# The last part of a convolution, attention and expert kernel issued in a written-out cyclic order

## The chip, the cores and the metric

The kernel runs on one core of a Trainium2 chip. The metric is the device time of one execution in microseconds. The kernel before took 6046.41 us, the median of three runs from 6041.91 to 6047.18. The core has five engines that work in parallel, each through its own list of instructions in order: TensorE (PE; its weight loads are shown apart as PEld), VectorE (DVE), ScalarE (ACT), GpSimd (POOL) and SyncE (SP), which in this kernel issues nearly all DMA transfers. An engine waits for another through semaphores.

## The reference

The input is 32 images of 128 channels and 64 x 64 pixels, float32. What is computed, cut to what matters:

```
# layer 0: group norm, then a convolution through learned butterfly transforms
x = x + conv(group_norm(x), weight, kd1, kd2, k11, k12, k21, k22)
#   x_f  = K11 . x . K12            (64 x 64 complex matrices along h and w)
#   prod[b, o, h, w] = sum_i x_f[b, i, h, w] * w_f[o, i, h, w]
#   out  = real(K21 . prod . K22)
# layer 1, on tokens t[b, pixel, channel]
k, v   = ln(t) @ Wk.T + bk, ln(t) @ Wv.T + bv
scores[b, e, f] = sum over pixels of k[b, pixel, e] * v[b, pixel, f]     # 128 x 128, one per image
t      = t + (softmax(scores / sqrt(32)) over f, applied to the channels of ln(t))
p      = softmax(ln(t) @ router_w + router_b)      # 8 experts, the best 2 kept, renormalised
t      = t + sum over the kept experts of gate * (ln(t) @ expert_w[e] + expert_b[e])
```

The attention matrix of an image is thus formed from all its 4096 tokens before it is applied to any of them; `ln` is a layer norm over the channels, taken anew for the experts.

## The kernel before, in words

The kernel has three parts, each of them a list of operations on tiles that a planner (class `Plan`, line 25) orders and then issues.

Part one transforms each image along w and h and leaves the spectrum in DRAM (`xf`). Part two goes over the 64 frequencies along w, mixes channels with the transformed weights and leaves the product in DRAM (`pf`). Part three, from line 853 on, is the one that is changed. It goes over the 32 images. For each image b it

- loads eight pieces `r0` to `r7` of the product (`load_r`, line 881; two DMAs of 256 KB each, on SP, line 887) and the input image `x` (`load_x`, line 877; 2 MB, on SP, line 879). A piece lies in one of ten buffers: pool `rp` with eight and `rp2` with two;
- transforms back along w: `w0` to `w7` on TensorE read one piece each (line 903, tile `pu`), and two copies to `u` for each half follow on ScalarE (`wo{e}_0`, `wo{e}_1`, line 913). All `w` share one PSUM tile of two banks, so a `w` waits for the `wo` of the one before;
- transforms back along h: `h0` to `h3` on TensorE (line 925, tile `py`), added to the image on VectorE (`ho0` to `ho3`, line 933). For the first two images these two steps are cut in halves (`w{e}_0`, `w{e}_1`, `h{g}_0`, `h{g}`; lines 946 and 965) in other PSUM buffers;
- turns the image to tokens in eight groups: `pt` on TensorE, `to` on ScalarE, `sa` (statistics) on VectorE; then `va`, `pwa` (a power on POOL) and `na` give the first layer norm;
- normalises (`xg`, ScalarE), forms the Gram matrix (`pg`, TensorE), and goes through a chain of small operations to the attention matrix (`gs pb t1 pb2 sm pr sr sn pc prx`);
- applies it to three token groups at a time: `pp` (TensorE), `at` (ScalarE), `ad` (VectorE, with the statistics of the second norm);
- norms again (`vb`, `pwb` on POOL, `nb`) and computes the router: `lg l2 f1 f2 f3 f4 f5 gt`, nearly all on VectorE, where `f1` and `f3` find the best and the second expert and `gt` makes the gates;
- runs the experts: for each of eight groups `xn` (normalise, ScalarE), `px` (transpose, TensorE) and `xT` (copy, ScalarE); for each of 32 token tiles two products `pe{i}_0`, `pe{i}_1` (TensorE, line 1324), each weighed by its gates on VectorE (`m{i}_0`, `m{i}_1`, line 1335); `s` on POOL sums the experts of two token tiles into the tokens; at last `st` (transpose back, TensorE), `so` (copy, ScalarE, line 1376) and the store to DRAM, which `so` issues on SP (line 1377).

Several images are in work at once: while the experts of image b run, image b + 1 is in its attention and image b + 2 or b + 3 in its transform back. `pe` has three PSUM buffers, and the tiles `px pt st pg pb pc pp` share three more.

Which operation comes when is the planner's choice. Each is added with an engine, a guessed duration, a due time and what must come before it (`after`); tokens of limited number (`take`, `free`) stand for buffers. `Plan.run` plays the program through with those guesses: each engine takes of its ready operations that with the earliest due time whose tokens are there. Due times are `SLOT` (114 us) times a position in images, shifted by a table for each kind of operation:

```
    def add(b, key, engine, us, at, run, after=(), take=(), free=(), late=0.0):
        names = [k if isinstance(k, tuple) else (b, k) for k in after]
        at += SHIFT.get(key.rstrip("0123456789_"), 0.0)
        made[b, key] = plan.add(
            engine, us, SLOT * at, run, [made[k] for k in names if k[0] >= 0], take, free, late
        )
```

The order that comes out is the order in which all operations are issued, and so the order of each engine's instructions. Loads and stores share the list of SP: a load of `r` waits there for its buffer, a store for the copy of `so`.

Of the kernel before, what the change touches and what calls it, by code (L numbers as in the profile page):

```python
# [19 lines left out]
NT = NPIX // P  # L20
# [4 lines left out]
class Plan:  # L25
# [12 lines left out]
    def run(self):  # L38
        ops, room = self.ops, self.room
        left = [len(set(o[4])) for o in ops]  # L40
        then = [[] for _ in ops]
        for i, o in enumerate(ops):
            for j in set(o[4]):
                then[j].append(i)
        ready = {o[0]: [] for o in ops}
        for i, o in enumerate(ops):
            if not left[i]:
                heapq.heappush(ready[o[0]], (o[2], i))
        busy = {e: False for e in ready}
        events, order, now = [], [], 0.0  # L50
        while True:
            for e, heap in ready.items():
                if busy[e]:
                    continue
                passed = []
                while heap:
                    due, i = heapq.heappop(heap)
                    take = ops[i][5]
                    if all(room[k] > 0 for k in take):
                        for k in take:  # L60
                            room[k] -= 1
                        order.append(i)
                        busy[e] = True
                        heapq.heappush(events, (now + ops[i][1], 0, i))
                        break
                    passed.append((due, i))
                for p in passed:
                    heapq.heappush(heap, p)
            if not events:
                break  # L70
            now, kind, i = heapq.heappop(events)
            engine, us, due, run, after, take, free, late = ops[i]
            if kind == 0:
                busy[engine] = False
                heapq.heappush(events, (now + 0.15 + late, 1, i))
            else:
                for k in free:
                    room[k] += 1
            for j in then[i]:
                if (kind == 0) == (self.quick and ops[j][0] == engine):  # L80
                    left[j] -= 1
                    if not left[j]:
                        heapq.heappush(ready[ops[j][0]], (ops[j][2], j))
        assert len(order) == len(ops)
        self.length = now
        for i in order:
            ops[i][3]()

# [2 lines left out]
def kernel(  # L91
# [16 lines left out]
    B = x.shape[0]  # L108
# [707 lines left out]
    NG = 4  # L816
# [12 lines left out]
    def prepare():  # L829
# [20 lines left out]
        nc.tensor.matmul(pe[:, 0:NE], om, prx[0][:, P + NE : QX], start=True, stop=True)  # L850
        nc.vector.tensor_scalar_mul(rws, pe[:, 0:NE], float(P))

    plan = Plan({"cv": 1, "pe": 3, "tl": 3, "r": 10, "x": 2, "xg": NG, "xn": 2, "xT": 2, "tm": 2, "so": 2, "gate": 2})
    SLOT = 114.0

    SHIFT = {
        "ad": -0.15, "at": -0.25, "f": 0.71, "gs": -1.97, "gt": 0.71, "h": -0.24, "ho": -3.5, "kvp": 3.43,
        "kvq": -0.45, "l": 0.71, "lg": 3.61, "m": -0.32, "na": -1.87, "nb": -0.81, "pb": -1.97, "pc": -1.97,
        "pe": 0.16, "pg": -0.08, "pp": 0.19, "pr": -1.97, "prx": -1.97, "pt": -0.23, "pwa": -1.87, "pwb": 3.61,
        "px": 0.15, "r": -0.04, "s": 0.08, "sa": 1.29, "sm": -1.97, "sn": -1.97, "so": 2.13, "sr": -1.97,  # L860
        "st": 1.1, "t": -1.97, "to": 0.06, "va": -1.87, "vb": 3.61, "w": 0.28, "x": -0.68, "xT": -0.68,
        "xg": 0.21, "xn": 2.42,
    }
    made = {}

    def add(b, key, engine, us, at, run, after=(), take=(), free=(), late=0.0):


        names = [k if isinstance(k, tuple) else (b, k) for k in after]
        at += SHIFT.get(key.rstrip("0123456789_"), 0.0)  # L870
        made[b, key] = plan.add(
            engine, us, SLOT * at, run, [made[k] for k in names if k[0] >= 0], take, free, late
        )


    def transfers(b):
        def load_x():
            xs[b] = xp.tile([P, HW, HW], F32, tag="x", name=f"y{b}")
            nc.sync.dma_start(xs[b].rearrange("c h w -> c (h w)"), xv[b])

        def load_r(e):
            def run():
                i = 8 * b + e
                ring, tag = (rp, "r") if i % 10 < 8 else (rp2, "r2")
                t = rs[b, e] = ring.tile([P, 16 * n], F32, tag=tag, name=f"r{b}_{e}")
                for r in range(2):
                    nc.sync.dma_start(t[r * n : (r + 1) * n], pfv[b, e, r])
            return run

        for e in range(8):  # L890
            add(
                b, f"r{e}", "SP", 0.2, b - 0.5 + 0.08 * e, load_r(e) if b else (lambda: None), take=("r",),
                late=5.0 if b else 0.0,
            )
        add(b, "x", "SP", 0.1, b + 0.2, load_x if b else (lambda: None), take=("x",), late=12.0 if b else 0.0)

    def conv(b):
        def w_inverse(e):
# [79 lines left out]
        if b < 2:  # L978
            for e in range(8):
                at = b + 0.08 * e  # L980
                for oh in range(2):
                    add(
                        b, f"w{e}_{oh}", "PE", 0.95, at + 0.04 * oh, w_inverse_piece(e, oh),
                        [f"r{e}"] + [(b - 1, f"h{k}") for k in range(4)], ("pe",), ("r",) if oh else (),
                    )
                    add(
                        b, f"wo{e}_{oh}", "ACT", 0.65, at + 0.04 * oh, w_out_piece(e, oh), [f"w{e}_{oh}"], (), ("pe",),
                    )
            for g in range(4):
                for k in range(2):  # L990
                    at = b + 0.68 + 0.07 * g + 0.035 * k
                    h, ho = (f"h{g}", f"ho{g}") if k else (f"h{g}_0", f"ho{g}_0")
                    add(
                        b, h, "PE", 1.05, at, h_inverse_piece(2 * g + k),
                        [f"wo{e}_{oh}" for e in range(8) for oh in range(2)] + ([f"h{g}_0"] if k else []), ("pe",),
                    )
                    add(b, ho, "DVE", 0.7, at, h_out_piece(2 * g + k), [h, "x"] + ([f"ho{g}_0"] if k else []), (), ("pe",))
            if b == 0:
                add(b, "prep", "PE", 3.5, 0.98, prepare, ["h3"], ("pe",), ("pe",))
            return  # L1000
        for e in range(8):
            at = b + 0.08 * e
# [11 lines left out]
    def front(b):  # L1014
# [53 lines left out]
        for g in range(8):  # L1068
            at = s1 + 0.016 * g
            add(b, f"pt{g}", "PE", 0.48, at, turn(g), [(b - 2, f"st{g}")] + [f"ho{k}" for k in range(4)], ("tl",))  # L1070
            add(b, f"to{g}", "ACT", 0.55, at, turned(g), [f"pt{g}"], (), ("tl",))
            add(b, f"sa{g}", "DVE", 0.85, at, stats1(g), [f"to{g}"] + (["sa0"] if g else []))
        add(b, "va", "DVE", 1.7, s1 + 0.14, lambda: moments(1), [f"sa{g}" for g in range(8)])
        add(b, "pwa", "POOL", 5.5, s1 + 0.14, lambda: power(1), ["va"])

# [77 lines left out]

        at = s1 + 0.40
        add(b, "gs", "DVE", 0.3, at, gsum, ["pg7"], (), ("tl",))
        add(b, "pb", "PE", 0.35, at, kv1, ["gs"], ("tl",))
        add(b, "t1", "DVE", 0.3, at, kv1_out, ["pb"])
        add(b, "pb2", "PE", 0.35, at, kv2, ["t1"])
        add(b, "sm", "DVE", 0.5, at, soft1, ["pb2"])
# [45 lines left out]
        for j, lo in enumerate(range(0, NT, 3)):  # L1205
            m = min(3, NT - lo)
            at = s1 + 0.45 + 0.016 * j
            add(b, f"pp{lo}", "PE", 0.26 * m, at, product(lo, m), ["prx", (b - 1, "lg")], ("tl",), ("x",) if lo == 30 else ())
            add(
                b, f"at{lo}", "ACT", 0.4 * m + 0.2, at, scaled(lo, m),  # L1210
                [f"pp{lo}"] + (["at0"] if lo else []),
# [67 lines left out]
        at = s1 + 0.64  # L1279
        add(b, "vb", "DVE", 1.7, at, lambda: moments(2), [f"ad{lo}" for lo in range(0, NT, 3)])  # L1280
        add(b, "pwb", "POOL", 5.5, at, lambda: power(2), ["vb"])
        add(b, "lg", "DVE", 1.95, at, logits1, ["vb"])
        add(b, "nb", "DVE", 2.1, at + 0.1, nmr2, ["pwb", "lg"])
        add(b, "l2", "DVE", 1.95, at + 0.1, logits2, ["nb"], ("gate",))
        add(b, "f1", "DVE", 4.15, at + 0.1, lambda: first_max(0), ["l2"])
        add(b, "f2", "DVE", 0.4, at + 0.1, second, ["f1"])
        add(b, "f3", "DVE", 4.15, at + 0.1, lambda: first_max(1), ["f2"])
# [4 lines left out]
    def experts(b):  # L1292
# [87 lines left out]
        s2 = b + 2  # L1380
        for g in range(8):
            at = s2 + 0.125 * g
            add(b, f"xn{g}", "ACT", 1.65, at - 0.1, normal(g), ["nb"], ("xn",))
            add(b, f"px{g}", "PE", 0.48, at - 0.05, turn(g), [f"xn{g}"], ("tl", "xT"), ("xn",))
            add(b, f"xT{g}", "ACT", 0.55, at - 0.05, turned(g), [f"px{g}"], (), ("tl",))
            for k in range(4):
                i = 4 * g + k
                for half in range(2):
                    add(
                        b, f"pe{i}_{half}", "PE", 0.86, at + 0.125 * (2 * k + half) / 8, expert(i, half), [f"xT{g}"],  # L1390
                        ("pe",), ("xT",) if k == 3 and half else (),
                    )
                    add(
                        b, f"m{i}_{half}", "DVE", 1.45 if i // 2 in direct else 0.64, at + 0.125 * (2 * k + half) / 8,
                        weighed(i, half) if i // 2 in direct else gated(i, half),
                        [f"pe{i}_{half}", "gt"] + ([f"m{i - k % 2}_0"] if k % 2 or half else []),
                        ("tm",) if k % 2 == 0 and half == 0 and i // 2 not in direct else (),
                        ("pe",) + (("gate",) if i == NT - 1 and half else ()),
                    )
                if k % 2 and i // 2 in direct:  # L1400
                    made[b, f"s{i // 2}"] = made[b, f"m{i}_1"]
# [8 lines left out]
    for b in range(B):  # L1410
# [1 line left out]
        conv(b)  # L1412
        front(b)
        experts(b)
    plan.run()


# [51 lines left out]
```

## Time and profile before

| what | us |
|---|---|
| median of 3 runs | 6046.41 |
| the profiled execution | 6034.45 |
| its span, first to last instruction | 6032.7 |
| part three, from about 2537 to the end | 3496 |
| TensorE busy in the span | 5884.8 (98%) |
| VectorE busy | 4220.6 (70%) |
| POOL busy | 4205.9 (70%) |
| ScalarE busy | 3757.1 (62%) |
| mean granted TensorE clock | 0.994 |

A row of the page's costly groups gives line, engine and operation, the tiles written and read with their shapes, how many there were, their busy time and the mean of one in ns, then the idle time of the engine just before them and what ended most of it. In a timeline each row has start, length, engine, line, operation, tiles and count, and in brackets the idle time before it and its releaser. "SPq" is SP's DMA queue: its rows show when a transfer was issued and how long issuing took, not when it landed. A wait is put down to what came last by the profile.

### The profile page before, as it was taken

Reading aid. Unit: us, or ns where it says so; the run is one execution under the profiler, and the core shown is the slowest. Engines: PE = TensorE matmul, PEld = TensorE weight load, DVE = VectorE, ACT = ScalarE, POOL = GpSimd, SP = SyncE. Lnnn points to the kernel's source line nnn. Section 1 sums busy time; section 2 is a strip of 40 time slices with the busy share of each in tenths; the row PEclk is TensorE's granted clock in tenths of the full one; section 3 lists DMA queues with packets and bytes.
Section 4 is the critical chain, followed back from the end, with each engine's and each line's share of the span. In section 5 each row is a group of like instructions: output and inputs, shape, how many; then the busy total and the mean of one; then the engine's idle time right before and its main releaser. Section 6 shows DMA issues by size and latency. Waiting matters only on the chain.

```text
span 6032.7 us, 219314 instructions
## 1 busy us (share of the span) xinstructions
PE 5884.8 (98%) x95372; PEld 4672.1 (77%) x95372; DVE 4220.6 (70%) x7696; ACT 3757.1 (62%) x7057; POOL 4205.9 (70%) x3793
## 2 busy tenths in 40 slices
PE   7999999999999999989999999999999999999998
PEld 7999999999999999866666666666666666666654
DVE  5565545555555555458778787887878788787888
ACT  7666664555555555467766676676767666676663
POOL 2110006666666666538898998989899888998988
PEclk9999999999999999999999999999999999999999
DMA  5767766666666666632222122221322222132100
GB/s 198 240 226 236 236 217 192 174 172 173 171 173 173 171 173 172 171 102 88 81 71 98 57 98 71 83 86 57 106 63 91 78 74 95 57 100 70 66 27 28
DMA packets 554068, 756.74 MB, mean 125 GB/s; under 512 B 58320, under 2 KB 318928, under 8 KB 549008
## 3 DMA queue, kind: packets, MB, share of 16 engines
q1 hardware_dynamic: 550496, 733.64, 40.3%
q8 instruction: 749, 12.27, 0.9%
q0 software_dynamic: 2608, 9.06, 0.5%
q14 instruction: 215, 1.76, 0.1%
HBM read 406.79 MB, written 335.54 MB: 123 GB/s over the span
## 4 chain that ended last, share of the span: by engine, by line
PE 88%; ACT 7%; issue 2%; DVE 1%; POOL 1%; DMA 1%; SPq 0%; POOLq 0%; ACTq 0%; DVEq 0%
PE pe L1324 28%; PE m L658 17%; PE g L636 9%; PE pf L418 7%; PE pu L903 6%; PE pp L1173 4%; PE py L925 4%; PE pg L1100 4%; PE pv L396 3%; PE px L1311 2%; ACT xn L1301 2%; ACT u L913 2%; PE pz L373 1%; ACT z L383 1%; PE pt L1049 1%
## 5 line engine op out<-in xcount | busy, mean ns | idle before, releaser
L1324 PE MATMUL pe<-ew_sb,xT 128*128 128x512 f32 x4096 | 1946.1, 597 | 19.4 <-DVE tm L1335 16.0
L1335 DVE TENSOR_TENSOR tm<-pe,oh 128x512 f32<-128x512 f32 x2028 | 1346.4, 684 | 479.3 <-PE pe L1324 455.5
L1360 POOL TENSOR_TENSOR tm<-tm 128x512 f32<-128x512 f32 x1014 | 1286.1, 1284 | 201.1 <-DVE tm L1335 182.7
L1324 PEld LDWEIGHTS pe<-ew_sb,xT 128*128 128x128 f32 x4096 | 700.9, 191 | 522.9 <-issue 396.1
L647 DVE COPY f<-g 128x1024 f32<-128x1024 f32 x508 | 622.2, 1225 | 648.9 <-PE g L636 648.9
L658 PE MATMUL m<-f,s 128*64 128x64 f32 x32768 | 1070.1, 224 | 1.9 <-issue 1.1
L658 PEld LDWEIGHTS m<-f,s 128*64 128x64 f32 x32768 | 1000.0, 138 | 63.2 <-issue 2.6
L604 POOL COPY s<-l 128x512 f32<-128x512 f32 x512 | 546.0, 1099 | 524.9 <-issue 508.3
L647 ACT COPY f<-g 128x1024 f32<-128x1024 f32 x508 | 514.5, 1013 | 561.0 <-PE g L636 534.8
L1363 POOL TENSOR_TENSOR tk<-tk,tm 128x256 f32<-128x256 f32 x1014 | 753.6, 743 | 79.5
L1361 POOL TENSOR_TENSOR tm<-tm 128x512 f32<-128x512 f32 x507 | 650.4, 1283 | 39.8
L913 ACT COPY u<-pu 64x512 f32<-64x512 f32 x960 | 556.6, 580 | 135.1 <-PE pu L903 121.5
L636 PE MATMUL g<-c,wst 9*128 9x128 f32 x16256 | 599.9, 283 | 3.6 <-issue 3.3
L636 PEld LDWEIGHTS g<-c,wst 9*128 9x128 f32 x16256 | 502.8, 186 | 38.5 <-issue 3.9
L349 POOL TENSOR_TENSOR grstd<-gms,mhalf 128x1 f32<-128x1 f32 x32 | 17.8, 555 | 735.8 <-DVE gms L345 735.8
L1186 ACT ACTIVATE pp<-pp,m 128x128 f32<-128x128 f32 x1024 | 440.9, 431 | 124.1 <-PE pp L1173 99.3
L606 POOL TENSOR_SCALAR s<-l 128x512 f32<-128x512 f32 x256 | 509.5, 1990 | 0.0
L903 PEld LDWEIGHTS pu<-qw,r 128*128 128x128 f32 x3840 | 455.7, 193 | 63.3 <-ACT u L913 49.5
L903 PE MATMUL pu<-qw,r 128*128 128x128 f32 x3840 | 476.3, 278 | 25.6 <-ACT u L913 25.6
L1317 ACT COPY xT<-px 128x512 f32<-128x512 f32 x256 | 150.2, 587 | 560.5 <-PE px L1311 557.5
L418 PE MATMUL pf<-ph,v 128*128 128x128 f32 x4096 | 491.0, 278 | 5.0 <-ACT z L383 1.1
L418 PEld LDWEIGHTS pf<-ph,v 128*128 128x128 f32 x4096 | 466.9, 192 | 14.7 <-ACT z L383 7.1
(177 smaller groups left out, 8573.0 us busy)
## 6 DMA issues: line engine op xcount, KB each, us to landing
xf<-f SPq DMA_DIRECT2D x512, 256.0 KB
pf<-o SPq DMA_DIRECT2D x1016, 128.0 KB
l<-xf SPq DMA_DIRECT2D x1012, 128.0 KB
r<-pf SPq DMA_DIRECT2D x496, 256.0 KB
x<-in_x_dram SPq DMA_DIRECT2D x256, 256.0 KB
out_dram<-so SPq DMA_DIRECT2D x256, 256.0 KB
y<-in_x_dram SPq DMA_DIRECT2D x31, 2048.0 KB
r<-pf POOLq DMA_DIRECT2D x16, 248.0 KB, 7.7
```

Of the source, the lines that this page charges most:

```text
L418: nc.tensor.matmul(pl[:, j * P : (j + 1) * P], vs[b][:, 8 * g + j, :], ph.rearrange("h r m -> h (r m)"), start=True, stop=True,)
L604: nc.gpsimd.tensor_copy(dst, src)
L636: nc.tensor.matmul(pg[g // 2][:, g % 2, m * P : (m + 1) * P], wst[rows, 16 * half + 4 * t + m, :], c[rows].rearrange("r h k -> r (h k)"), ...
L647: copy(f.rearrange("i m (g o) -> i m g o", g=2), tile_of["g", w, half, t][k].rearrange("i g (o m) -> i m g o", o=4))
L658: nc.tensor.matmul(ps[hh * n : (hh + 1) * n, q, :], s[:, h].rearrange("i k b -> i (k b)")[:, B * r : B * r + n], f[:, h, r, :], start=(r = ...
L903: nc.tensor.matmul(ps[:, k, :], rs[b, e][:, k * P : (k + 1) * P], qw.rearrange("w r m -> w (r m)"), start=True, stop=True,)
L913: nc.scalar.copy(u[r * n : (r + 1) * n, :, oh * n + 8 * e : oh * n + 8 * e + 8], ps[oh * n : (oh + 1) * n, :, r * n : (r + 1) * n].rearran ...
L1324: nc.tensor.matmul(ps, tile_of["xT", b, i // 4][:, i % 4, :], ew_sb[:, es, :].rearrange("d e c -> d (e c)"), start=True, stop=True,)
L1335: nc.vector.tensor_tensor(tile_of["tm", b, i // 2][:, i % 2, es, :], tile_of.pop(("pe", b, i, half)).rearrange("p (e c) -> p e c", c=P), t ...
L1360: nc.gpsimd.tensor_tensor(tm[:, k, 0:4, :], tm[:, k, 0:4, :], tm[:, k, 4:8, :], ALU.add)
L1361: nc.gpsimd.tensor_tensor(tm[:, :, 0:2, :], tm[:, :, 0:2, :], tm[:, :, 2:4, :], ALU.add)
L1363: nc.gpsimd.tensor_tensor(t[:, lo : lo + 2, :], t[:, lo : lo + 2, :], tm[:, :, m, :], ALU.add)
```

## The change

Part three is no longer drawn by the planner. A new method `Plan.follow` takes a finished order, asserts that dependencies and tokens hold at each step, and issues the operations in it. The order is written out as one cycle of 322 words, each an operation with a stage: the operation of image b gets the position b + stage + (place in the cycle) / 322. For the first two and the last two images a table `EDGE` shifts the position of each kind of operation. Positions are sorted, and that is the order. `SHIFT` is dropped. Tokens `x`, `xT`, `so` and `gate` are dropped too, and where one of them held two operations apart an explicit `after` is added instead. `prep` of image 0 (the folding of norms into the weights) comes after that image's `va`, and what reads its results now names it.

```
+    def follow(self, order):
+        ops, room, done = self.ops, dict(self.room), set()
+        for i in order:
+            for k in ops[i][5]:
+                room[k] -= 1
+            assert done.issuperset(ops[i][4]) and min(room.values()) >= 0, i
+            for k in ops[i][6]:
+                room[k] += 1
+            done.add(i)
+        assert len(done) == len(ops) == len(order)
+        for i in order:
+            ops[i][3]()
...
-    plan = Plan({"cv": 1, "pe": 3, "tl": 3, "r": 10, "x": 2, "xg": NG, "xn": 2, "xT": 2, "tm": 2, "so": 2, "gate": 2})
+    plan = Plan({"cv": 1, "pe": 3, "tl": 3, "r": 10, "xg": NG, "xn": 2, "tm": 2})
...
-        at += SHIFT.get(key.rstrip("0123456789_"), 0.0)
...
-        add(b, "x", "SP", 0.1, b + 0.2, load_x if b else (lambda: None), take=("x",), late=12.0 if b else 0.0)
+        add(b, "x", "SP", 0.1, b + 0.2, load_x if b else (lambda: None), [(b - 2, f"pp{lo}") for lo in range(0, NT, 3)], late=12.0 if b else 0.0)
...
-            if b == 0:
-                add(b, "prep", "PE", 3.5, 0.98, prepare, ["h3"], ("pe",), ("pe",))
...
+        if b == 0:
+            add(b, "prep", "PE", 3.5, 1.2, prepare, [f"sa{g}" for g in range(8)], ("pe",), ("pe",))
...
+            last = [(b - (g < 2), f"pe{4 * ((g - 2) % 8) + k}_{half}") for k in range(4) for half in range(2)]
             add(b, f"xn{g}", "ACT", 1.65, at - 0.1, normal(g), ["nb"], ("xn",))
-            add(b, f"px{g}", "PE", 0.48, at - 0.05, turn(g), [f"xn{g}"], ("tl", "xT"), ("xn",))
-            add(b, f"xT{g}", "ACT", 0.55, at - 0.05, turned(g), [f"px{g}"], (), ("tl",))
+            add(b, f"px{g}", "PE", 0.48, at - 0.05, turn(g), [f"xn{g}"], ("tl",), ("xn",))
+            add(b, f"xT{g}", "ACT", 0.55, at - 0.05, turned(g), [f"px{g}"] + last, (), ("tl",))
...
-    plan.run()
+    ORDER = """
+        m24_1:4 m26_0:4 lg:3 m27_1:4 sa0:2 r6:0 r0:0 r3:1 r2:1 r4:1 r7:1 x:1 r1:0 r5:1 pwb:3 pe26_1:4 pe25_0:4
+        pe27_0:4 w2:1 m26_1:4 m25_0:4 nb:3 m27_0:4 l2:3 f1:3 pe28_0:4 pe28_1:4 st4:4 st5:4 pt2:2 pe29_0:4 wo2_0:1
+        wo2_1:1 xn0:3 so5:4 so4:4 to2:2 s12:4 s13:4 m28_0:4 m28_1:4 m29_0:4 f2:3 w3:1 px0:3 pt4:2 pt5:2 pe29_1:4
...
+        pe24_0:3 pp18:2 pe25_1:3 pp30:2 w0:0 at21:2 at18:2 at30:2 wo0_0:0 wo0_1:0 s11:3 s10:3 m24_0:3 ad21:2 ad18:2
+        ad30:2 vb:2 m25_1:3 pe24_1:3 st0:3 pe26_0:3 pt0:1 w1:0 pe27_1:3 px7:3 to0:1 wo1_0:0 wo1_1:0 xT7:3 so0:3
+    """
+    EDGE = {
+        0: """
...
+            pt:-0.3123 pwa:-0.2116 pwb:0.0030 px:0.0132 r:-0.3851 sa:-0.2796 sm:0.0039 sn:0.0118 so:-0.0034
...
+        B - 2: """
...
+            px:-0.0207 r:-0.0021 s:0.0020 sa:-0.0108 sm:-0.0069 sn:0.0017 so:-0.0224 sr:0.0005 st:-0.0072
...
+        B - 1: """
...
+            pt:-0.0029 pwa:-0.0001 pwb:-0.0700 px:-0.0470 r:-0.1228 s:0.0070 sa:0.0001 sm:-0.0001 sn:0.0010
+            so:0.1625 sr:0.0020 st:0.0941 t:0.0044 to:-0.0054 va:-0.0045 vb:0.0035 w:0.0027 wo:-0.0015 x:-0.0514
...
+    edge = {b: {k: float(s) for k, s in (w.split(":") for w in words.split())} for b, words in EDGE.items()}
+    turns, words = [], [w.split(":") for w in ORDER.split()]
+    for p, (key, stage) in enumerate(words):
+        for b in range(B):
+            keys = [key]
+            if b < 2 and key[0] == "w" and key[1:].isdigit():
+                keys = [key + "_0", key + "_1"]
+            elif b < 2 and key.rstrip("0123456789") in ("h", "ho"):
+                keys = [key + "_0", key]
+            elif b == 0 and key == "va":
+                keys = [key, "prep"]
+            for z, k in enumerate(keys):
+                if (b, k) in made:
+                    at = b + int(stage) + p / len(words) + edge.get(b, {}).get(k.rstrip("0123456789_"), 0.0)
+                    turns.append((at + (1e-5 if k == "prep" else z * 1e-6), made[b, k]))
+    plan.follow(list(dict.fromkeys(i for at, i in sorted(turns))))
```

## The prediction

> **What bounds the kernel now.** I read the page's busy table first, then busy time by stage, the chain of waits, one period of the timeline of TensorE and of SP, and SP's own waits.
>
> ```profile
> PE 5884.8 (98%) x95372; PEld 4672.1 (77%) x95372; DVE 4220.6 (70%) x7696; ACT 3757.1 (62%) x7057; POOL 4205.9 (70%) x3793
> ```
> ```profile
> 2537.00:2747.00 210.00, 182.55 (x2444) 146.15 (x2441) 110.74 (x300) 127.18 (x289) 86.04 (x79) 0.96 0.42 120
> 2747.00:5832.00 3085.00, 3043.63 (x21513) 2078.78 (x21512) 2479.79 (x5479) 2113.68 (x4837) 2763.77 (x2383) 1.00 0.24 77
> 5832.00:6033.00 201.00, 168.49 (x585) 88.32 (x584) 163.35 (x345) 78.59 (x188) 175.19 (x154) 0.94 0.08 29
> ```
> The rows are stretches of the last part (columns: length, busy PE, PEld, DVE, ACT, POOL, clock, DMA share, GB/s). In the middle one TensorE is busy 98.7%: it is the bound. It is periodic, one image a turn:
>
> ```profile
> 2852.74 5.15 PE pe L1324 x12
> ...
> 5724.84 5.15 PE pe L1324 x12
> ```
> The same piece of the chain recurs 27 periods later, so a period is 2872.1/27 = 106.37 us. From starts in one period (4022.7 to 4129.1) I take the time TensorE spends on each kind with nothing in its way: 64 expert products at 0.86 (55.0), 8 `w` at 1.79 (14.3), 4 `h` at 2.02, products 7.8, Gram 7.1, 24 groups of transposes at 0.44 (10.5), small ones 0.7: 103.5. So 2.9 us a period is lost: about 0.9 in changing to and from `h`, 2.0 in waits such as
>
> ```profile
> 4034.02 2.05 PE L903 MATMUL pu<-qw,r 128*128 128x128 f32 x16 [0.53 <-ACT u L913]
> 4051.24 0.66 PE L1049 MATMUL pt<-ident,y 128*128 128x128 f32 x4 [0.79 <-ACT tk L1054]
> ```
> A better order has 2.0 us a period to win. What it can lose is seen on SP:
>
> ```profile
> 4115.84 1.08 SPq L887 DMA_DIRECT2D r<-pf  x2
> 4118.78 0.35 SPq L879 DMA_DIRECT2D y<-in_x_dram  x1
> 4122.72 1.09 SPq L887 DMA_DIRECT2D r<-pf  x2
> 4127.70 0.34 SPq L1377 DMA_DIRECT2D out_dram<-so  x1
> 4128.82 1.08 SPq L887 DMA_DIRECT2D r<-pf  x2
> ```
> ```profile
> SPq L887 <- PE pu L903: 62.8, 2, 59.3
> SPq L1377 <- ACT so L1376: 23.7, 6, 5.5
> ```
> Loads of `r` (two DMAs each), the load of `x` and the stores `so` go out on one queue, in just the order in which the program lists them, and SP stands at each until its wait is over, 59.3 us once. Today that is harmless: a load waits for a buffer and is issued about one period before the `w` that reads it.
>
> **What the Trainium skill says.** "DMA: Bandwidth & Descriptors", section "Anatomy of one DMA — SWDGE (gpsimd) path": a semaphore wait of a DMA is done on the issuing sequencer before dispatch, not by the DMA engines. The rows above agree: no issue overtakes another. Same page, "Queues, rings and completion order": each DMA engine takes descriptors in ring order, so I let loads issued together land one after another; no row here shows two landings. "TensorE: Matmul & The Clock Gate", section "What's actually happening": after an idle window of about 3.4 us TensorE's clock is halved until it has been busy about as long. The trace agrees: after 5.04 us of idling six matmuls took 4.73 us, elsewhere 2.74.
>
> ```profile
> 5827.53 2.74 PE L1324 MATMUL pe<-ew_sb,xT 128*128 128x512 f32 x6
> ...
> 5863.45 4.73 PE L1324 MATMUL pe<-ew_sb,xT 128*128 128x512 f32 x6 [5.04 <-DVE tm L1335]
> ```
>
> **The change part by part.** No instruction is added or removed on any engine; only their order changes. Tokens (`x`, `xT`, `so`, `gate`) become explicit `after` lists: free. `prep` moves from before `pt0` of image 0 into the `w` pieces of image 1. In the trace TensorE waits 2.33 us there for VectorE and then runs at clock 0.50; with the 2.0 us of such a restart (above) I book 4 us gained.
>
> Reading the new ORDER by engine: TensorE, ScalarE and VectorE keep nearly the old cycle, with groups 2 and 6 permuted. The waits above lose their causes, but new ones appear: with VectorE's rows laid end to end from `ad0` on, `pe29_1` comes 0.5 us before `m28_0` (behind `f1`, 3.7 us) has freed its PSUM buffer, and `pe1_0` 0.8 us before `m1_1` (behind `gt`, 3.65). Their sum, 1.3, is the upper end and 0.3 the lower, if the starts are off by 0.5 each; I take 0.8. Alone, that gives 103.5 + 0.9 + 0.8 = 105.2 us, 1.2 less than now.
>
> SP decides. In ORDER the loads stand together: `r6:0 r0:0 r3:1 r2:1 r4:1 r7:1 x:1 r1:0 r5:1` at words 5 to 13 of 322; the word before them on SP's queue is the store in `so0`, the last of the cycle. `r2:1` stands 10 words ahead of its reader `w2:1` (word 18), the same image. So:
>
> 1. On ScalarE `so0` follows `wo1_0 wo1_1 xT7`, which need `w1`. `w1` ends at 0.
> 2. ScalarE: 0.2 us to start, four copies 2.35, `xT7` and `so0` 1.15: `so0` ends at 3.7. Rows:
>
> ```profile
> 4052.60 1.95 PE L903 MATMUL pu<-qw,r 128*128 128x128 f32 x16
> 4052.90 1.08 ACT L1376 COPY so<-po 128x512 f32<-128x512 f32 x2
> ...
> 4054.58 2.35 ACT L913 COPY u<-pu 64x512 f32<-64x512 f32 x4 [0.60 <-PE pu L903]
> ```
> 3. SP issues the store (0.34, and 0.1 to the next): the first load goes out at 4.15.
> 4. `r2` is the fourth. One load of 524 KB issued at 4136.63 moved its last byte near 4141.0: 4.4 us.
>
> ```profile
> 4138.00:4139.00 1.00, 0.98 (x10) 0.77 (x8) 0.96 (x2) 0.98 (x3) 1.00 (x2) 1.00 0.49 127
> 4139.00:4140.00 1.00, 0.86 (x8) 0.61 (x6) 0.97 (x2) 0.96 (x3) 1.00 (x1) 1.00 0.71 229
> 4140.00:4141.00 1.00, 0.61 (x5) 0.61 (x6) 1.00 (x3) 0.97 (x3) 0.92 (x2) 1.00 0.47 152
> ```
> With the DMA engines full such loads run at 246 GB/s (2582 to 2584, share 1.04): 2.13 us each. Three more: 6.4. `r2` lands at 4.15 + 10.8 = 14.95; with 0.2 to start, `w2` begins at 15.15.
> 5. TensorE has between `w1` and `w2` only four expert products and one transpose group, 3.9 us. It stands still 15.15 − 3.9 = 11.25 us.
> 6. The half clock after it: 4.73 − 2.74 = 2.0.
>
> Queued behind `w2` on TensorE is the rest of the image; all of it shifts, and with it the next `w1` and so the next `so0`: the stall can't be absorbed, it is a loop once a period. While TensorE stands, VectorE, ScalarE and POOL catch up, so the 0.8 of new waits vanishes. Behind `so0` on SP stand all nine loads; `r3` lands before `r2`; `r4` and `r7` 2 and 4 us after, needed 11 and 32 later; `r5`, behind `x` (2 MB), about 14 after, needed at 19: hidden. The slot rings (8 + 2) hold: at worst `r5` waits for `w2`.
>
> New period: 103.5 + 0.9 + 0.3 (ScalarE at `w1`) + 11.25 + 2.0 = 117.95, 11.6 more. Bounds: if loads move at twice the rate, so that issue (4 × 1.09) and 3.3 us after it are the limit, landing takes 7.7, not 10.8; without the clock loss, +6.5. If the eight DMAs in flight share the engines evenly, the last of `r2`, issued at 4.4, needs eight times 1.07 and lands at 13; if the clock costs 3.4 (an estimate from the clock page: two windows of 3.4 us at half rate), that is +15.2.
>
> How many: images 0 to 2 load before any store exists; images 3 to 29 stand behind `so0` (27); image 30, with EDGE, has `r3 r2` behind it (4.3 less: +7.3); image 31 loads before `so0`. 27 × 11.6 + 7 = 320. The fill brings −4; the drain is taken as 0 and may be 20 off either way, as its 32 us of idle TensorE (201 − 168.5) are neither clearly kept nor removed. Against the profiled execution (6034.45; span 6032.7, 1.7 us around it): 6034 + 316 = 6350; the median of the runs (6046.41) is 12 above it: 6362, rounded to 6360.
>
> **Rivals.** (a) *The loads are not held by the store*, TensorE alone bounds the last part: 105.2 a period, 28 × 1.2 = 34 and 4 of the fill gained: 6046 − 38 = 6008. For it: the old order loses 2.0 a period to waits that the new one avoids. Against: SP's rows. It decides if `so0` could be issued some 11 us earlier, or if SP's instructions were put in another order than listed. That would also be the case of a change that doesn't do what it says. (b) *Held, but briefly*: fast landing and no clock loss, 27 × 6.5 + 3: 6225. For it: 229 GB/s at share 0.71 in a row above means 320 at full share. Against: the fill. (c) *Held, and more goes late*: the stores' two `so` buffers wait for stores queued behind `x`, so `wo4` or `f5` on ScalarE comes late, another 4 us a period: 6034 + 27 × 15.6 + 15 + 12 = 6480. Against: by the sum above `so5` lands some 2 us before `so6` wants its buffer.
>
> **How the numbers follow.** Forecast 0.70, (a) 0.12, (b) 0.10, (c) 0.07; no change in sum 0.01. The forecast's own range, from a step of ±4 us a period, is 6250 to 6470. With (b) and part of (c) 6200 to 6490; (a) stays outside. Under about 0.2% (12 us) this kernel's runs tell nothing apart; so faster 0.12, same 0.01, slower 0.87.
>
> **What would show it.** Right: in every period a TensorE idle of 9 to 13 us before `pu` (L903) released by a DMA of `r`, SP with nine loads in a row just after a store, a clock near 0.5 after the idle, a period near 118, and a first part that is unchanged. Wrong: SP's loads issued half a period before their `w`, TensorE still above 98%; or an idle that VectorE or ScalarE ends.

## The result, and the profile after

The changed kernel takes 6432.84 us (median of 4 runs, 6430.5 to 6434.14) against 6045.44 us for the kernel before (a fourth run is in this median): 1.0641 times as long, 95% interval 1.0623 to 1.066. The profiled execution spans 6432.4 us (6032.7 before).

The busy row of the page, and its row for the `w` matmuls (busy, mean ns, then the idle time ahead of them and what ended it); the last row is that of the kernel before:

```profile
PE 5954.7 (93%) x95372; PEld 4738.5 (74%) x95372; DVE 4252.7 (66%) x7696; ACT 3765.1 (59%) x7057; POOL 4213.6 (66%) x3793
...
L907 PE MATMUL pu<-qw,r 128*128 128x128 f32 x3840 | 521.3, 294 | 345.1 <-DMA r<-pf 336.8
...
L903 PE MATMUL pu<-qw,r 128*128 128x128 f32 x3840 | 476.3, 278 | 25.6 <-ACT u L913 25.6
```

TensorE does the same 95372 instructions, its share falls from 98% to 93%, and 336.8 us of idling stand ahead of one operation, ended by the DMA that brings `r`. Before, no `w` waited for a load. By stage (columns as in the table of before):

```profile
2537.00:2770.00 233.00, 192.21 (x2813) 154.81 (x2809) 127.03 (x320) 132.09 (x296) 104.08 (x98) 0.95 0.36 99
2770.00:5832.00 3062.00, 2731.49 (x18887) 1886.86 (x18887) 2197.68 (x4798) 1866.93 (x4245) 2419.65 (x2076) 0.94 0.23 71
5832.00:6433.00 601.00, 545.94 (x3213) 344.05 (x3209) 464.64 (x1008) 331.83 (x777) 513.54 (x450) 0.96 0.16 51
```

In the middle TensorE is busy 89% of the time (98.7% before) at a clock of 0.94 (1.00). The chain of waits between the last work ahead of the stall and the work after it, at one ordinary turn (start, length, engine, what is written, line, count; "issue" is time in which the engine waits for nothing that the profile shows):

```profile
4302.16 1.72 PE pe L1328 x4
...
4312.34 1.78 PE pu L907 x16
...
4316.72 1.92 PE pu L907 x16
...
4321.63 0.50 ACT so L1380
4322.14 0.33 SPq L1381
...
4322.56 0.45 SPq L891
...
4326.90 7.82 DMA r<-pf
4334.72 0.14 issue
4334.86 3.75 PE pu L907 x16
4338.61 2.42 PE pe L1328 x4
```

`w1` ends, ScalarE comes to `so0`, SP issues its store, then the loads; `r2`, the fourth, lands at 4334.7 and only then does `w2` run. Its 3.75 us against the 1.78 of another `w`, and the 2.42 us of the next four expert products against 1.72, are the halved clock: the record has 0.50 from 4326.3 to 4339.8. SP's own timeline of this turn shows the cause in five rows:

```profile
4233.05 89.42 SPq L1381 DMA_DIRECT2D out_dram<-so  x6
4322.56 8.56 SPq L891 DMA_DIRECT2D r<-pf  x12
4331.75 0.35 SPq L883 DMA_DIRECT2D y<-in_x_dram  x1
4332.71 7.02 SPq L891 DMA_DIRECT2D r<-pf  x4
4343.32 26.80 SPq L1381 DMA_DIRECT2D out_dram<-so  x6
```

For 89 us SP goes from store to store, and all eight loads and `x` go out in 17 us after `so0`. Its waits say the same of the whole run (who waited, for whom, then us in total, times, longest):

```profile
SPq L1381 <- ACT so L1380: 3096.1, 191, 71.6
SPq L891 <- PE po L1374: 71.0, 5, 14.5
```

The second row, a load that waits for TensorE five times (run 5 below names the operation), is not in the sum of the prediction. It belongs to the longer turn that comes once in five images; the chain shows turns of 118.68, 119.45, 119.43, 126.75, 119.61 and 119.11 us here:

```profile
4133.86 5.15 PE pe L1328 x12
4252.54 5.15 PE pe L1328 x12
4371.99 5.15 PE pe L1328 x12
4491.42 5.15 PE pe L1328 x12
4618.17 5.15 PE pe L1328 x12
4737.78 5.15 PE pe L1328 x12
4856.89 5.15 PE pe L1328 x12
```

Over 26 turns (2813.39 to 5939.40) the mean is 120.23 us; an ordinary one has 119.03, the fifth about 125.3. Before, every turn had 106.37.

### The profile page after: what moved, and what is told of

Its sections match the earlier page's. It is cut to its first block, busy times and chain, and to the rows that moved or that the text cites. A ratio compares the mean times of both kernels' runs of the same rounds, so it can differ in the third digit from the quotient of the medians.

```text
span 6432.4 us, 219323 instructions
## 1 busy us (share of the span) xinstructions
PE 5954.7 (93%) x95372; PEld 4738.5 (74%) x95372; DVE 4252.7 (66%) x7696; ACT 3765.1 (59%) x7057; POOL 4213.6 (66%) x3793
## 4 chain that ended last, share of the span: by engine, by line
PE 85%; ACT 4%; DMA 4%; DVE 2%; SPq 2%; issue 2%; POOL 1%; ACTq 0%; DVEq 0%; POOLq 0%
PE pe L1328 25%; PE m L671 16%; PE g L649 9%; PE pu L907 8%; PE pf L431 7%; PE py L929 4%; PE pp L1177 4%; PE pg L1104 4%; DMA r<-pf 3%; PE pv L409 3%; SPq L891 2%; PE pt L1051 2%; PE po L1374 2%; PE px L1315 2%; PE pz L386 1%
## 5 line engine op out<-in xcount | busy, mean ns | idle before, releaser
L1328 PE MATMUL pe<-ew_sb,xT 128*128 128x512 f32 x4096 | 1982.6, 602 | 22.1 <-DVE tm L1339 17.4
L907 PE MATMUL pu<-qw,r 128*128 128x128 f32 x3840 | 521.3, 294 | 345.1 <-DMA r<-pf 336.8
L907 PEld LDWEIGHTS pu<-qw,r 128*128 128x128 f32 x3840 | 504.8, 208 | 442.8 <-issue 411.4
L1093 ACT ACTIVATE xg<-tk,m 128x128 f32<-128x128 f32 x1024 | 403.9, 480 | 162.1 <-DVE m L1083 93.4
```

The lines of the kernel that those rows point to most:

```text
L907: nc.tensor.matmul(ps[:, k, :], rs[b, e][:, k * P : (k + 1) * P], qw.rearrange("w r m -> w (r m)"), start=True, stop=True,)
L1328: nc.tensor.matmul(ps, tile_of["xT", b, i // 4][:, i % 4, :], ew_sb[:, es, :].rearrange("d e c -> d (e c)"), start=True, stop=True,)
```

## The experiments

The theory: the order of computing is a small gain, the place of the loads behind the store of `so0` is the whole loss. The rival: TensorE, ScalarE and VectorE are slower in the new cycle, whatever the loads do. Runs 1 to 4 were measured beside 6048.34 us for the kernel before, runs 5 to 7 beside 6048.09 us.

**1. The store of `so0` moved behind most loads.** Only SP's order differs, `so0` itself being the last of the cycle on ScalarE:

```
+                    if k == "so0":
+                        at += 13.5 / len(words)
```

> The changed kernel with the store of so0 listed 13.5 words later, between r1 and r5; every engine but SP keeps its order. If the place of the loads behind that store is the cause: the idle before w2 (12.4 us) and the half clock after it (2.0) go, an ordinary period falls from 119.2 to about 105, every fifth keeps its extra 5 us (r5 still waits for a buffer ahead of the stores), in sum 6433 - 27 x 14.2 = about 6045 (6010 to 6060). If the new order of TensorE, VectorE and ScalarE is itself the slow part, or eight loads in one burst: little changes, above 6380.

6046.46 us, 0.9997 of before (0.9988 to 1.0005). 386 of the 387 us went with one store's place on one queue. The row of `w`:

```profile
L907 PE MATMUL pu<-qw,r 128*128 128x128 f32 x3840 | 475.4, 277 | 8.8 <-ACT u L917 8.8
```

No idling for a DMA is left, and a mean of 277 ns where the changed kernel has 294: the slow clock went too. It is not the burst of loads that costs: here six of them still go out at once (12 DMAs in 8.84 us from 4006.43), but 33 us ahead of that store (4039.73). The ordinary turn is 104.9 us, 1.5 less than before the change, but every fifth still has some 111.

**2. The stores issued by ScalarE.**

```
-                nc.sync.dma_start(ov[b][:, g * 512 : (g + 1) * 512], so)
+                nc.scalar.dma_start(ov[b][:, g * 512 : (g + 1) * 512], so)
```

> The changed kernel with the stores of so issued by ScalarE instead of SP. If the loads are late only because SP stands at a store: they now go out as soon as buffers are free, no idle before w2, the extra 5 us of each fifth period go as well since no store stands behind r5, about 105 a period, 6433 - 27 x 15.4 = about 6015 (5990 to 6040), TensorE's loss to ScalarE's eight issues included. If the burst or the compute order is the cause: above 6380.

6035.56 us, 0.9977 (0.9968 to 0.9986). With the loads alone on SP no store stands ahead of them. The turn is 105.6 us and no long one is left. The time lies in the upper part of the expected range; where the 0.7 us a turn over run 1's ordinary ones go was not traced.

**3. `r2` and `r3` first among the loads.** The store still stands ahead.

```
-r6:0 r0:0 r3:1 r2:1 r4:1 r7:1 x:1 r1:0 r5:1
+r2:1 r3:1 r6:0 r0:0 r4:1 r7:1 x:1 r1:0 r5:1
```

> The changed kernel with r2 and r3 ahead of r6 and r0 in the burst of loads. If w2 waits for the landing of the fourth load: r2 as the first lands 4.6 us after the store instead of 12.2, the idle falls from 12.4 to about 4.9 us, the clock still drops or nearly so, 7.5 a period, 6433 - 203 = about 6230 (6200 to 6260). If what counts is the burst as a whole (eight loads that share the engines and land together): r2 lands at 8 or later, above 6330.

6404.05 us, 1.0584 (1.0568 to 1.0599): a miss. The number lies where the rival had it, but not for the rival's reason: `r2` landed 6.2 us after its issue (4314.70 to 4320.91), neither at 4.6 nor with the whole burst at 8 or later. The wait at `w2` halved, 174.1 us over 28 turns, 6.2 each, and another came:

```profile
PE pu L907 <- DMA r<-pf: 174.1, 28, 6.7
PE px L1315 <- ACT so L1380: 104.0, 29, 6.0
```

The chain of one turn names it:

```profile
4315.20 5.71 DMA r<-pf
4320.92 9.56 DMA r<-pf
4330.55 12.35 DMA out_dram<-so
...
4343.64 0.96 PE px L1315 x4
```

The store of `so5`, issued behind nine loads, lands 12.35 us after its issue, 28.6 after the store of `so0`; ScalarE's `so6` needs its buffer, and `px` on TensorE waits for ScalarE. Here `so6` could have started at 4338.4 and waited 4.6 us. In the changed kernel `w2`, and with it `so6`, comes 6 us later, and no wait of it for the store shows in an ordinary turn: the two waits lie side by side, and taking one away uncovers the other. The idles together are 6.2 + 104.0/28 = 9.9 us a turn instead of 12.4, but each is followed by a slow clock, and the mean turn is 119.08: all that was gained, 29 us, is the long turns. About 1 us of this balance is not placed.

**4. The old order of computing, with `so0` and the nine loads put just ahead of `w2`.** In the kernel before, for images 0 to 26 of `so0`:

```
+            order = [i for i in order if i not in group]
+            p = order.index(made[k + 3, "w2"])
+            order[p:p] = group
```

> The kernel before, its planned order kept on TensorE, VectorE and POOL, with so0 and the nine loads in the changed kernel's sequence moved to just before w2 for images 3 to 29. If the place of the loads alone makes the change's loss: st0 stands 3.9 us after w1 there, so so0 ends about 0.7 us after w2's place, 0.45 + 12.2 later r2 has landed: an idle of about 13 us and 2 of clock, less the 2.0 that such an idle covers, and some of the fifth periods' extra: 13 to 15 a period, 6046 + 27 x 14 = about 6420 (6380 to 6460). If the new compute order is to blame: about 6046.

6538.48 us, 1.0809 (1.0791 to 1.0827). TensorE, VectorE and POOL keep the old order here; on ScalarE the copy of `so0` moves along with its store. By this one move the old order loses as much as the new one, and more, so the new order is not needed for the loss; the size was missed by 118. Its row of `w`:

```profile
L910 PE MATMUL pu<-qw,r 128*128 128x128 f32 x3840 | 534.2, 298 | 431.5 <-DMA r<-pf 363.8
```

363.8 us over 27 turns are 13.5 each. Ordinary turns are about 122.4 us (16.0 more than before), six have about 131.6 (25.3 more): 21 × 16.0 + 6 × 25.3 = 488. The expected 6420 was 27 turns of some 14, without the longer ones. In one of these a load waited 17.1 us for TensorE, as in the changed kernel; their cause was not tested apart here.

**5. `r6` loaded one turn later, in the place of `r1`.** The profile of a long turn of the changed kernel (the timelines of SP, of ScalarE and of TensorE) suggested why:

```profile
4570.66 0.35 SPq L883 DMA_DIRECT2D y<-in_x_dram  x1
4571.66 19.10 SPq L891 DMA_DIRECT2D r<-pf  x4
4590.81 25.48 SPq L1381 DMA_DIRECT2D out_dram<-so  x6
```
```profile
4596.05 0.59 ACT L1380 COPY so<-po 128x512 f32<-128x512 f32 x1 [5.20 <-DMA out_dram<-so]
```
```profile
4596.69 1.11 PE L1315 MATMUL px<-ident,xn 128*128 128x128 f32 x4 [4.02 <-ACT so L1380]
```

Pieces whose number `8b + e` ends in 8 or 9 live in a pool of two. Once in five images that pool holds `r6` of the next image and `r4` of this one when `r5` is to be loaded, so the load waits on SP for `w4` (14.2 us in the mean), and the stores of `so5` and `so4` stand behind it. (The row of waits names a transpose that follows `w4` on TensorE; `w4` starts at 4587.70 and takes 1.8 us, and the load goes out at 4589.68.) If `r6` is loaded a turn later, the pool has room.

```
-r6:0 r0:0 r3:1 r2:1 r4:1 r7:1 x:1 r1:0 r5:1
+r0:0 r1:0 r3:1 r2:1 r4:1 r7:1 x:1 r6:1 r5:1
```

> The changed kernel with r6 loaded one period later, in the place of r1, and r1 in the place of r6; r2 stays the fourth load behind the store. So at most eight pieces are held when the loads go out, and none waits for a buffer. Theory: the ordinary period stays at 119.1 us with 12.4 us of idle before w2, the extra 6.2 us of every fifth goes, 5 or 6 times: about 6398, range 6388 to 6410. Rival (the fifth has another cause): 6432.

6409.05 us, 1.0601 (1.0587 to 1.0615). All turns are alike, 119.42 us in the mean of 26: the long ones are gone, and so is SP's wait of a load for `w4`. The gain is 24 us, not 34, since the ordinary turn grew by 0.4; the idling ahead of `w2` grew from 336.8 to 350.3 us over 28 turns, and why was not traced.

**6. Run 3 with `x`, `r1` and `r5` behind the stores of `so5` and `so4`.**

```
-r2:1 r3:1 r6:0 r0:0 r4:1 r7:1 x:1 r1:0 r5:1
+r2:1 r3:1 r6:0 r0:0 r4:1 r7:1
...
-so5:4 so4:4
+so5:4 so4:4 x:1 r1:0 r5:1
```

> As the run with r2 first among the loads, but x, r1 and r5 stand behind the stores of so5 and so4 on SP. Theory: there the store of so5, 28.6 us behind so0's because nine loads stood ahead of it, took back what r2 had won; behind six loads of 2.1 us each it lands before ScalarE asks for its buffer, so the wait of 6.0 us at px goes and the idle of 6.2 us before w2 stays: period near 113, about 6240, range 6200 to 6300. Rival (what w2 wins returns through something other than the store's place): 6390 to 6410.

6288.85 us, 1.0396 (1.0382 to 1.041), 115 less than run 3. The wait at `px` falls from 104.0 us to 3.9 (two times); so the place of the stores behind the loads was what took back the gain of run 3. The turn is 115.1 us, not 113, because now `r5`, behind the 2 MB of `x`, lands late for `w5` in most turns. TensorE's timeline of one turn:

```profile
4265.21 3.75 PE L907 MATMUL pu<-qw,r 128*128 128x128 f32 x16 [6.41 <-DMA r<-pf]
...
4288.72 2.61 PE L907 MATMUL pu<-qw,r 128*128 128x128 f32 x16 [2.02 <-DMA r<-pf]
```

**7. Each load put just behind the `w` nine pieces earlier.** The computing is in the new order; there are ten buffers, so the one wanted is free when the load's turn comes.

```
+                    if b and k[0] == "r" and k[1:].isdigit():
+                        q, e = divmod(8 * b + int(k[1:]) - 9, 8)
+                        at = q + where[f"w{e}"] + edge.get(q, {}).get("w", 0.0) + 2e-6
```

> The changed kernel with its order of computing as it is, but each load of r follows, on SP, the w nine pieces earlier, so that its buffer is free when it is listed and it has most of a period to land. Theory (the order of computing is a gain, and the loads' place alone the loss): no TensorE idle at w2, no longer period in every fifth image, period 104.9 us, 28 x 1.5 us below the kernel before: about 6006, range 5990 to 6020, which is rival (a) of the prediction. Rival (the longer fifth period does not come from r5's buffer, or the order itself costs elsewhere): about 6040 or more.

6003.99 us (6001.65 to 6008.82), 0.9931 of before (0.9918 to 0.9943): faster than both kernels, by little but clear of noise. Its busy row and stage table:

```profile
PE 5892.5 (98%) x95372; PEld 4686.1 (78%) x95372; DVE 4281.6 (71%) x7696; ACT 3762.2 (63%) x7057; POOL 4205.4 (70%) x3793
```
```profile
2745.00:5805.00 3060.00, 3055.06 (x21598) 2096.56 (x21597) 2555.21 (x5521) 2129.01 (x4856) 2773.94 (x2385) 1.00 0.26 79
```

In the middle TensorE is busy 99.8% of the time, and a turn takes 104.92 us, with no long one. In the kernel before no `w` waited for a load either, so the 44 us (6048.09 − 6003.99) are what the order of computing is worth, start and end included, and the place of the loads costs about 430.

## Why the prediction was right, point by point

The forecast was 6360 with 6200 to 6490; measured 6432.84. In the ordinary turn the mechanism is the one forecast, step for step; the longer turns were not forecast. The growth was 73 us more than the sum had.

- **Steps 1 to 3** (`w1`, `so0`, issue). `so0` ends 3.5 us after `w1` (4318.64 to 4322.12; forecast 3.7), the first load goes out at 3.9 (4.15). Right.
- **Step 4** (landing) was mis-sized. `r2` landed 12.2 us after the first load's issue, not 10.8. The term that failed is the first load's 4.4 us: it was read from a load issued alone, and is when its last bytes moved. In run 3, where `r2` is first behind the store and seven more loads follow at once, it took 6.2 us to its landing. How the 1.8 us divide between the store ahead, the loads behind and the time from the last bytes to the landing was not taken apart. Each further load costs (12.2 − 6.2)/3 = 2.0, as forecast (2.13). In the sum the turn shown idles for 12.36 us instead of 11.25.
- **Step 5.** Work between `w1` and `w2` as forecast (3.9 us).
- **Step 6** (clock) was also too small. `w2` loses 3.75 − 1.78 = 1.97 us, the forecast's 2.0, but the four products after it lose 2.42 − 1.72 = 0.70 more. Without stall and clock the turn shown would be 119.45 − 12.36 − 2.67 = 104.4; the forecast had 104.7. Runs 1 and 7 measured 104.9 for the new order alone, near the forecast's 105.2, and run 7's 6004 us is near its 6008 for rival (a). Its 0.8 us of new waits are hardly seen, though: in run 7 TensorE stands for some 0.2 us a turn (4.9 us in 3060). The mean ordinary turn is 119.03 us against 117.95: 26 × 1.08 = 28 us.
- **"The slot rings hold: at worst `r5` waits for `w2`"** was wrong. Once in five images it waits for `w4`, and the stores behind it make ScalarE late: the chain that rival (c) names, set off by another wait, in a fifth of the turns. In the trace that is (120.23 − 119.03) × 26 = 31 us; run 5 had none of these turns and was 24 us faster, with a somewhat longer ordinary turn.
- **Rival (c) in the ordinary turn** was rejected by 2 us of slack at `so6`. Run 3 shows how thin that was: with `w2` 6 us earlier, ScalarE waited 4.6 us there. In the changed kernel `so6` starts 29.8 us after the store of `so0` (4322.14 to 4351.89); if the store of `so5` landed after 28.6 as in run 3, the slack was about 1 us, an estimate.
- **Fill, drain and image 30.** From the last matmul of the second part (2536.6 us before, 2547.8 after) to the end, the profiled execution grew by 388.6 us: 26 turns × 13.86 = 360, and 28 for the rest. The forecast had some 15 there (one more ordinary turn and the 7 of image 30, less the fill's 4). Image 30 itself came nearly as forecast, with a shorter idle than the other 27: 8.1 us, where 11.25 − 4.3 = 7.0 follow from the forecast. The remainder was not taken apart. The second part is the same in both kernels; over the nine profiles here it ends between 2536.6 and 2551.9, earliest in the kernel before.

The 28 us of the ordinary turns, the 31 of the long ones and some 13 of this rest make up the 73, within 1. These three go the same way, so it was not luck that large errors cancelled. It was not a rival that came true: (b), with no clock loss and fast landing, is excluded by the 3.75 us and the 12.2.

## What to carry to other kernels

On a queue that issues in order, a load inherits every wait that is listed ahead of it: a store of the last result just ahead of the next inputs joins the end of one turn to the start of the next, and only the loads' lead over their readers can hide that. List a load right behind what frees its buffer (here nine pieces ahead of its reader), or give stores another issuing engine, and only then judge an order of computing: the one here was a gain of 0.7% that looked like a loss of 6.4%. Count buffers by pool and not in sum, since one pool that is full once in five images holds all that stands behind it.

## What the runs showed of the hardware

A load of 524 KB (two DMAs) issued alone had moved its last bytes 4.4 us after its issue. The first of eight loads issued right behind a store landed after 6.2 us (run 3), and one in fourth place after 12.2 (the changed kernel): 2.0 us for each load ahead of it. A store of 262 KB issued on the same queue behind 6.3 MB of loads took 12.35 us to land (run 3, issued at 4330.55). By the rows below some 3.5 MB of the loads had moved by then, an estimate (5 us at 197, 247 and 252 GB/s). The DMA share in the last two rows was 1.04 to 1.08 at about 250 GB/s:

```profile
4315.00:4320.00 5.00, 0.00 (x0) 0.00 (x0) 4.83 (x8) 0.00 (x0) 4.76 (x6) 0.99 0.78 197
4320.00:4325.00 5.00, 3.96 (x17) 3.91 (x18) 2.55 (x3) 0.17 (x1) 4.76 (x5) 0.50 1.04 247
4325.00:4330.00 5.00, 5.00 (x22) 2.94 (x21) 1.62 (x3) 4.91 (x11) 1.62 (x2) 0.82 1.08 252
```

The same rows show the clock that "TensorE: Matmul & The Clock Gate", section "What's actually happening", of the Trainium skill describes: 0.50 after an idle of 6.4 us, then recovering. What one such stretch costs is not read from the first operation after the idle alone. In the turns shown `w2` takes 3.75 us after 12.4 us of idling and after 6.4 alike, but the slow clock lasts into the products behind it, and for how long differs from turn to turn: in run 3 the four products after `w2` took from 1.9 to 3.1 us. Nor did it take the idle window of about 3.4 us that the forecast cited from that section: in run 6 an idle of 2.02 us ahead of `w5` was followed by a clock of 0.50 from 4290 to 4293. There `w5` took 2.6 to 3.7 us after the five idles of 2.0 to 2.9 us, and 2.0 us after idles of up to 1.8.
